# Seven block products for two output classes of an MLP's second product, with their differences on GpSimd

## The chip, the core and the metric

The kernel runs on one core of a Trainium2 chip. The core has a matrix engine (TensorE, PE in the profile; its weight loads are PEld), a vector engine (VectorE, DVE), an activation engine (ScalarE, ACT), GpSimd (POOL) and a queue engine for transfers (SyncE, SP). They run side by side; each takes its own instructions strictly in the order in which they are written, and an instruction that needs another engine's result waits on a semaphore. TensorE reads SBUF and accumulates in PSUM, which has eight banks of 512 float32 columns; VectorE and ScalarE read PSUM, GpSimd does not.

The metric is the device time of one execution in microseconds. All data are float32.

## The reference

The input is 16 images of 192 channels and 64 x 64 pixels. Cut to what matters here:

```python
h  = ln2d(x)                                   # over channels
projected, gate = split(conv1x1(h, in_proj))   # 192 -> 2 x 192
projected = dwconv3(projected)
mixed = (scan_4_directions(projected) + dwconv3(projected)) * sigmoid(gate)
x = x + conv1x1(gelu(batchnorm(mixed)), out_proj)
h2 = ln2d(x)
m = conv1x1(gelu(conv1x1(h2, fc1) + b1), fc2) + b2    # 192 -> 768 -> 192
x = x + m                                      # "the image"
# second layer: per-image 3x3 taps of which 4 are unmasked
pooled = mean(x, axis=(2, 3))
taps = relu(norm(pooled @ w1.T)) @ w2.T + b2
out = depthwise_conv3x3(x, taps per image and channel, masked) + bias
```

The change concerns `conv1x1(gelu(...), fc2)`, the second MLP product, and the buffers that hold the image between it and the last convolution.

## The kernel before

The kernel has three stages. The first normalizes and projects the input, the second runs the depthwise convolutions and scans channel by channel, the third does everything from the batch norm on. The order of all instructions on all engines is the order in which the program writes them; no scheduler moves anything.

**Layout of the third stage.** Two images are worked on at once, one on partitions 0 to 63 and one on 64 to 127 (`HALF`). The 192 channels are three classes of 64 (`t` = 0, 1, 2). A step `n` handles one chunk of 512 pixels (8 rows) of a pair of images; a pair has 8 steps, there are 8 pairs, 64 steps in all. In a step, the loop at L1141 writes work of four different chunks: the MLP of chunk `n`, the normalization of `n + 1`, the out-projection of `n + 2`, and the unmixing (transposes) and Gelu of the mixed data of `n + 3`.

**The MLP.** `first` (L965) makes one of six blocks of 128 hidden channels: twelve matmuls of 64 x 64 weights and 512 columns into a tile of two PSUM banks (tag `f1`, two such tiles), then ScalarE's Gelu into an SBUF tile `gl` of 128 x 2 x 512 (six of them). `second` (L978) multiplies the six blocks with the three classes of `wf2`, 128 x 64 weights and 512 columns per image, through `both` (L840): 36 matmuls in a step. Each float32 matmul has two records in the profile, so 72. They accumulate in three PSUM banks (tag `f2`). `final` (L991), at the start of the next step, adds each class with its bias to the image on VectorE (L997) and lets the same instruction sum the pixels for the pooling.

**The normalization.** `residual` (L900) adds out-projection, bias and input into the image and collects channel sums (L910, L921). `mean`, `center`, `squares` and `normalize` produce `h`, the MLP's input: two matmuls against a constant matrix, a subtraction (L941), ScalarE's squares (L949) and their sums on VectorE (L950, L921), a square root on ScalarE (L959), a reciprocal (L962) and a scaling (L963) on VectorE.

**The last convolution.** When a pair has ended, its taps are computed (`pooled`, `squeeze`, `excite`) and its twelve pieces (four bands of 16 rows x three classes) are put on a list. `piece()` (L1075) takes one: ScalarE does the first tap (L1034), VectorE three more (L65), and GpSimd's queue stores the result (L1038). It is called twice a step, so the pieces of one pair fill the first six steps of the next.

**Buffers.** The images are held in two tiles `ximg` of 3 x 65 x 66 values a partition, one per pair in turn; row 0 and the side columns are zeros (`border`, L817). The second tile first serves as room for mixed data (`spare`, `ys`).

The order within a step of before: `final(n-1)`, `first` 0 and 1, `mean` and `center`, `first` 2, `squares`, `first` 3 and 4, `unmix`, `load_mixed`, a piece, `first` 5, the out-projection's matmuls (L890, L897) mixed with the second `mean`, `residual` of class 1, `normalize`, `residual` of 0 and 2, Gelu of the mixed data, `second`, with the second piece inside it. `second`'s order of matmuls is written at L985 to L989:

```python
order = [(m, t) for m in gl for t in range(3)]
for m, t in order:
    both(s["po"][t], lambda i: wf2[:, m, 64 * t:64 * t + 64], lambda i: gl[m][:, i], m == 0, m == NFC - 1)
```

Of the kernel before, what the change touches and what calls it, by code (L numbers as in the profile page):

```python
# [27 lines left out]
C = 192  # L28
# [27 lines left out]
def conv_block_kernel(ctx: ExitStack, tc: tile.TileContext, x, prm, w_in, w_out, w_fc1, b_fc1, w_fc2, w1, bn1, w2, out):  # L56
# [756 lines left out]
    n_img = 2  # L813

    ximg = [k3.tile([128, 3, HW + 1, RW], F32, tag=f"ximg{i}", name=f"ximg{i}") for i in (1, 0)][::-1]

    def border(xi):  # L817
        nc.gpsimd.memset(xi[:, :, 0:1], 0.0)
        nc.gpsimd.memset(xi[:, :, :, 0:1], 0.0)
        nc.gpsimd.memset(xi[:, :, :, RW - 1:RW], 0.0)  # L820


    spare = ximg[1].rearrange("p t h w -> p (t h w)")
    ys = {n // 2: spare[:, (n - 2) * 3 * CH:n * 3 * CH].rearrange("p (t w e) -> p t w e", t=3, w=2) for n in range(2, NCH, 2)}
    ys[0] = y_low
# [5 lines left out]
    wp = ctx.enter_context(tc.tile_pool(name="w2", bufs=1))  # L831
# [4 lines left out]
    NPS = NFC // 2  # L836
# [3 lines left out]
    def both(ps, w, rhs, start, stop):  # L840

        for i, q in enumerate(HALF):
            nc.tensor.matmul(ps[q], w(i), rhs(i), start=start, stop=stop)  # L843

    def img_of(n):
        r = 1 + (n % NCH) * CR
        return ximg[(n // NCH) % n_img][:, :, r:r + CR, 1:1 + HW]
# [52 lines left out]
    def residual(n, t, ps):  # L900
# [4 lines left out]
        if n == 0:  # L905
            return
        s["added"] = s.get("added", ()) + (t,)
        if t < 2 and len(s["added"]) == 2:
            s["sum"] = hp2.tile([128, 3, HCH], F32, tag="sm", name="sm", bufs=1)
            nc.vector.tensor_add(rows(s["sum"][:, 0:2].rearrange("p k n -> p (k n)")), img[:, 0], img[:, 1])  # L910
        if t == 2:
            sm = s["sum"]
            s["sm"] = [sm[:, j] for j in range(3)]
            sums(*(rows(sm[:, j]) for j in (0, 1, 2, 0, 1)), img[:, 2, 0:CR // 2], img[:, 2, CR // 2:CR])
# [30 lines left out]
    def squares(n):  # L945
# [3 lines left out]
        nc.scalar.activation(sq, s["h"], AF.Square)  # L949
        nc.vector.tensor_add(sq[:, 0], sq[:, 0], sq[:, 1])  # L950
# [4 lines left out]
    def normalize(n):  # L955
        s = st[n]
# [6 lines left out]
        nc.vector.tensor_mul(s["h"], s["h"], rs.unsqueeze(1).broadcast_to([128, 3, CH]))  # L963
# [14 lines left out]
    def second(n, k):  # L978
        s = st[n]
        gl = {m: s.pop(("gl", m)) for m in (2 * k, 2 * k + 1)}  # L980
        if k == 0:
            po = [ps2.tile([128, CH], F32, tag="f2", name="ps_f2", bufs=3) for _ in range(3)]

            s["po"] = po[1:] + po[:1]
            order = [(m, t) for t in range(3) for m in gl]  # L985
        else:
            order = [(m, t) for m in gl for t in range(3)]
        for m, t in order:
            both(s["po"][t], lambda i: wf2[:, m, 64 * t:64 * t + 64], lambda i: gl[m][:, i], m == 0, m == NFC - 1)  # L989

    def final(n):  # L991
        p, c = divmod(n, NCH)
        if c == 0:
            pst[p]["sums"] = hp2.tile([128, 3, NCH], F32, tag="sums", name="sums")
        img = img_of(n)
        for t in range(3):
            nc.vector.scalar_tensor_tensor(img[:, t], rows(st[n]["po"][t]), pt3[:, t, FC2B:FC2B + 1], img[:, t],  # L997
                                           ALU.add, ALU.add, accum_out=pst[p]["sums"][:, t, c:c + 1])
        st[n].clear()
# [27 lines left out]
    def dynamic(p, g, t):  # L1027
        xi, taps, r = ximg[p % n_img], pst[p]["taps"], g * GR
        o = op.tile([128, GR, HW], F32, tag="o", name="o")
        for k in range(NTAP):  # L1030
            src = xi[:, t, r + k // 3:r + k // 3 + GR, k % 3:k % 3 + HW]
            w = taps[:, t, k:k + 1]
            if k == 0:
                nc.scalar.activation(o, src, AF.Identity, bias=pt3[:, t, BIAS:BIAS + 1], scale=w)  # L1034
            else:
                stt(o, src, w, o)
        for i, q in enumerate(HALF):
            nc.gpsimd.dma_start(ov[2 * p + i, 64 * t:64 * t + 64, r * HW:(r + GR) * HW], o[q].rearrange("p h w -> p (h w)"))  # L1038

    def dynamic_last(p, r, nr, t, dg, o=None, queues=(nc.gpsimd, nc.sync)):  # L1040

        xi, taps, hr = ximg[p % n_img], pst[p]["taps"], nr // 2
        src = lambda k, r0, n: xi[:, t, r0 + k // 3:r0 + k // 3 + n, k % 3:k % 3 + HW]
# [29 lines left out]
    pieces = []  # L1073

    def piece():  # L1075
        if pieces:
            dynamic(*pieces.pop(0))
# [29 lines left out]
    border(ximg[0])  # L1107
# [29 lines left out]
    out_alone(1, 2)  # L1137
    idle(1)


    for n in range(n_ch + 1):  # L1141
        ended = (n - 1) // NCH if n >= NCH and (n - 1) % NCH == NCH - 1 else None
# [7 lines left out]
        if n == 1:  # L1150
            load_y(6, ys[3], (nc.gpsimd,))
        if n == NCH - 3:
            border(ximg[1])
        at(first, n, 0)
        at(first, n, 1)
# [4 lines left out]
        if n == 0:  # L1160
            unmix(2)
        at(first, n, 2)
        at(squares, n + 1)
        for m in range(3, NFC - 1):
            at(first, n, m)
            if n == 0 and m == 3:
                bn_gelu(2)
        at(unmix, n + 3)
        at(load_mixed, n + 4)
        piece()  # L1170
        at(first, n, NFC - 1)
# [21 lines left out]
        at(normalize, n + 1)  # L1193
        if po:
            for t in (0, 2):
                residual(n + 2, t, po[t])
        at(bn_gelu, n + 3)
        at(second, n, 0)
# [4 lines left out]
        at(second, n, 1)  # L1203
        piece()
# [77 lines left out]
```

## Time and profile before

| | |
|---|---|
| median of three runs | 3676.18 us (3673.29 to 3678.82) |
| profiled execution | span 3672.7 us from first to last instruction; its own time outside the span is not shown apart |
| third stage | from about 1328 us to the end, 64 steps |
| one step | 35.96 us |
| one step, busy | TensorE 35.96, VectorE 26.75, ScalarE 15.77, GpSimd 2.13 us |
| mean granted TensorE clock | 0.998 of full speed |

How the rows are read. A row of the groups has line, engine and operation, output <- inputs with shapes, the count, then busy microseconds and mean nanoseconds of one, then the engine's idle time before it and what ended it. A row of the timeline has start and length in microseconds, then the same. Matmul rows overlap each other (several run at once in different parts of the array), so the time of a run of matmuls is read from its start to the start of the row after it. The view of stages has for each window its length, and each engine's busy time with the number of instructions.

### The profile page before, as it was taken

The numbers are of one execution on the slowest core, as the hardware profiler recorded it, in microseconds if no ns is written. First come the engines' busy times: TensorE is split into PE (matmuls) and PEld (weight loads), VectorE is DVE, ScalarE is ACT, GpSimd is POOL, SyncE is SP. The second block draws the span as 40 slices with busy tenths as digits, with TensorE's granted clock in tenths as the row PEclk, the third lists the DMA queues.
The fourth block names the chain that finished last, engine by engine and source line by source line (L and its number), as shares of the span: only waits on it lengthen the run. The fifth ranks groups of instructions, "written<-read, shape, count | busy, mean of one in ns | idle before, by whom it ended". The sixth has DMA issues, their size and how long they took to land.

```text
span 3672.7 us, 71322 instructions
## 1 busy us (share of the span) xinstructions
PE 3649.8 (99%) x30354; PEld 1724.1 (47%) x30354; DVE 2713.3 (74%) x4138; ACT 1792.0 (49%) x2004; POOL 419.3 (11%) x685
## 2 busy tenths in 40 slices
PE   9999999999999999999999999999999999999998
PEld 6666666555566643343343334333334334333334
DVE  7878776999999965557757767776766775775764
ACT  3343434988888843334443534343444434343533
POOL 3434332111111120000000000000000000000000
PEclk9999999999999999999999999999999999999999
DMA  7898998999999951022212212222222231222212
GB/s 172 243 251 247 264 278 245 300 297 290 280 279 288 250 104 37 25 60 66 78 47 81 75 47 67 81 61 53 77 71 55 65 85 47 75 69 61 73 38 75
DMA packets 290334, 491.81 MB, mean 134 GB/s; under 512 B 26584, under 2 KB 184784, under 8 KB 290016
## 3 DMA queue, kind: packets, MB, share of 16 engines
q1 hardware_dynamic: 232540, 296.22, 30.2%
q0 software_dynamic: 56544, 189.99, 18.7%
q8 instruction: 239, 3.92, 0.5%
q10 hardware_dynamic: 932, 1.03, 0.1%
q14 instruction: 79, 0.65, 0.1%
HBM read 284.95 MB, written 197.92 MB: 131 GB/s over the span
## 4 chain that ended last, share of the span: by engine, by line
PE 90%; DVE 1%; DMA 0%; issue 0%; ACT 0%; ACTq 0%; SPq 0%; POOL 0%; DVEq 0%
PE ps_f L973 27%; PE ps_f L843 27%; PE ps_l L673 11%; PE ps_pj L514 7%; PE ps_d L629 7%; PE ps_o L897 5%; PE ps_o L890 2%; PE ps_xt L485 1%; PE ps_m L929 1%; PE ps_v L929 1%; PE ps_k L843 0%; DMA xa<-in_x_dram 0%; DVE o L65 0%; PE pb_h L141 0%; DVE ol L65 0%
## 5 line engine op out<-in xcount | busy, mean ns | idle before, releaser
L975 ACT ACTIVATE gl<-ps_f,bf 128x1024 f32<-128x1024 f32 x384 | 428.0, 1115 | 1298.5 <-PE ps_f L973 1292.8
L973 PE MATMUL ps_f<-h,wf 64*64 64x512 f32 x9216 | 1014.9, 590 | 2.0 <-DVE h L963 2.0
L843 PE MATMUL ps_f<-gl,place 128*64 128x512 f32 x4608 | 1001.9, 592 | 0.8 <-ACT rs L959 0.8
L973 PEld LDWEIGHTS ps_f<-h,wf 64*64 64x64 f32 x9216 | 346.3, 133 | 627.9 <-issue 566.0
L843 PEld LDWEIGHTS ps_f<-gl,place 128*64 128x64 f32 x4608 | 334.9, 137 | 623.8 <-issue 613.9
L514 PE MATMUL ps_pj<-wi,xa 64*128 64x384 f32 x3072 | 514.7, 487 | 1.7 <-DVE stg L519 1.2
L514 PEld LDWEIGHTS ps_pj<-wi,xa 64*128 64x128 f32 x3072 | 292.0, 187 | 196.0 <-issue 10.6
L65 DVE SCALAR_TENSOR_TENSOR o<-ximg,taps,o 128x1024 f32<-128x1024 f32 (+1 forms) x267 | 336.5, 1261 | 22.5 <-ACT o L1034 14.1
L941 DVE TENSOR_TENSOR h<-ximg,ps_m 128x768 f32<-128x768 f32 x128 | 116.4, 951 | 308.2 <-PE ps_m L929 307.0
L1038 POOL DMA_DIRECT2D out_dram<-o x168 | 89.8, 539 | 2012.5 <-DVE o L65 2009.7
L997 DVE SCALAR_TENSOR_TENSOR ximg<-ps_f,pt,ximg 128x512 f32<-128x512 f32 x192 | 144.4, 752 | 173.1 <-PE ps_f L843 160.4
L664 DVE TENSOR_TENSOR_SCAN v<-tab,q 128x1024 f32<-128x1024 f32 x96 | 218.3, 2274 | 7.8 <-ACT tab L652 7.8
L962 DVE RECIPROCAL rs<-rs 128x512 f32<-128x512 f32 x64 | 214.1, 3346 | 5.3 <-ACT rs L959 5.2
L666 DVE TENSOR_TENSOR_SCAN v<-tab,q 128x1024 f32<-128x1024 f32 x96 | 217.6, 2266 | 0.0
L520 ACT ACTIVATE mid<-ps_pj,rsa 128x384 f32<-128x384 f32 x128 | 120.2, 940 | 184.2 <-PE ps_pj L514 178.8
L652 ACT ACTIVATE tab<-mask,dec_b 128x1024 f32<-128x1024 f32 x192 | 209.8, 1146 | 0.0
L520 ACT ACTIVATE stg<-ps_pj,rsa 128x384 f32<-128x384 f32 x128 | 120.0, 941 | 180.4 <-PE ps_pj L514 172.9
L950 DVE TENSOR_TENSOR low<-low 128x512 f32<-128x512 f32 x63 | 43.6, 693 | 209.2 <-ACT low L949 209.2
L903 DVE SCALAR_TENSOR_TENSOR ximg<-ps_o,pt,low 128x256 f32<-128x256 f32 x384 | 168.1, 478 | 30.5 <-PE ps_o L897 28.0
L492 DVE BATCH_NORM_STATS2 st<-ps_xt 128x6 f32<-128x192 f32 x512 | 173.9, 340 | 13.8 <-PE ps_xt L485 13.0
L897 PE MATMUL ps_o<-low,wo 128*64 128x256 f32 x1536 | 182.0, 385 | 0.2 <-ACT low L870 0.2
L243 DVE STREAM_TRANSPOSE low<-low 128x512 f32<-128x512 f32 x174 | 170.0, 1029 | 2.0 <-issue 0.3
(213 smaller groups left out, 4186.1 us busy)
## 6 DMA issues: line engine op xcount, KB each, us to landing
low<-in_x_dram SPq DMA_DIRECT2D x128, 384.0 KB
out_dram<-o POOLq DMA_DIRECT2D x168, 256.0 KB, 4.6
mid<-pg_d SPq DMA_DIRECT2D x8, 4096.0 KB
low<-mixed_d SPq DMA_DIRECT2D x116, 256.0 KB
low<-pg_d SPq DMA_DIRECT2D x7, 4096.0 KB
pg_o<-pg_d SPq DMA_DIRECT2D x7, 4096.0 KB
xa<-in_x_dram POOLq DMA_DIRECT2D x192, 128.0 KB, 5.6
xa<-in_x_dram SPq DMA_DIRECT2D x192, 128.0 KB
```

Of the source, the lines that this page charges most:

```text
L65: nc.vector.scalar_tensor_tensor(o, in0, scalar, in1, ALU.mult, ALU.add, **kw)
L514: nc.tensor.matmul(ps[i], pixels(n, t, g)[q], wi[q, t].rearrange("p g k c -> p (g k c)"), start=(t == 0), stop=(t == 2))
L520: nc.scalar.activation(stag[blk][1][:, :, j], ps[1], AF.Copy, scale=rs[:, g, 1:2])
L629: nc.tensor.matmul(dst(ps[o, ih]), mats[g % 2]["dm"][q, di + 1, :, ch], src(s["pg"][q, :, 0, ch]), start=(di == 0), stop=stop)
L664: nc.vector.tensor_tensor_scan(vf, tab, q, 0.0, ALU.mult, ALU.add)
L666: nc.vector.tensor_tensor_scan(vf[:, ::-1], tab[:, ::-1], q[:, ::-1], 0.0, ALU.mult, ALU.add)
L673: nc.tensor.matmul(dst(bst[k]["ps"][o, i]), lm_of(g)[q, m, :, c], src(q, ih), start=start, stop=stop)
L843: nc.tensor.matmul(ps[q], w(i), rhs(i), start=start, stop=stop)
L897: nc.tensor.matmul(ps[wh][q].rearrange("p (r w) -> p r w", w=32), wo[:, 64 * t:64 * t + 64], cols(rows(s["mx"][:, i]))[:, :, wh], start=fi ...
L962: nc.vector.reciprocal(rs, rs)
L973: nc.tensor.matmul(pf[o, i], wf1[q, t, m0:m0 + 64], s["h"][q, t], start=(t == 0), stop=(t == 2))
L975: nc.scalar.activation(gl, pf, AF.Gelu, bias=bf1[:, m:m + 1])
```

## The change

The two output classes 0 and 1, with the hidden blocks 0 to 2 and 3 to 5 and the two halves of the 512 pixels, are written as a product of 2 x 2 block matrices, weights [[a11, a12], [a21, a22]] by hidden values [[b11, b12], [b21, b22]], in seven block products instead of eight (Winograd's form of Strassen's method). Class 2 stays as it was (`last_tile`).

- **Weights.** `sums_of_weights` makes four sums of weight blocks once, on GpSimd, before the first step.
- **Differences.** `differences` makes four differences of hidden blocks a step, each in three instructions of 128 x 512 on GpSimd: t1 = b12 - b11 and t2 = b22 - t1 while `first` makes the blocks; b12 = b22 - b12, in place, once the first half of class 2 has read it; b21 = b21 - t2, in place, once products 2 and the second half of class 2 have read it.
- **Products.** `seven` runs one block product: three blocks x two images, 256 columns. Products 1, 6, 7 and 4 accumulate in one bank (`chain`), which VectorE reads between them: 1 into class 0 left, 1+6 into class 0 right, 1+6+7 into class 1 right, 1+6+7+4 into class 1 left. Products 5, 2 and 3 use the two halves of a tile of the tag `f1`.
- **Additions.** `onto` adds a product to the image on VectorE: seven of 256 columns and one of 512 in place of three of 512.
- **Order.** `first` makes blocks 0, 3, 1, 4, 2, 5. `unmix` and `load_mixed` move to the start of the step, `residual` loses its channel sums to `add_up`, which comes after class 2's second half; `squares` and `normalize` are cut in two (`add_squares`; `spread_root` and `scale`). A piece's first tap on ScalarE comes at the end of the step before (`begin`), two or one in turn; its other taps come after blocks 0 and 4. The stores go to SP's queue.
- **Buffers.** Instead of two whole images, six slots of 17 rows (one row above and a band of 16) are used in turn; after each band GpSimd copies its last row to the top of the next slot, and `top` clears the first.

The order of `second` and the differences, cut from the diff (`n` is the step; the rest of the moves is told above):

```diff
+    def differences(n, m, kind):
+        b11, b12, b21, b22 = (quarter(n, k, x) for k, x in ((0, 0), (0, 1), (1, 0), (1, 1)))
+        if kind == 1:
+            sub(t1[:, m], b12(m), b11(m))
+        elif kind == 2:
+            sub(t2[:, m], b22(m), t1[:, m])
+        elif kind == 3:
+            sub(b12(m), b22(m), b12(m))
+        else:
+            sub(b21(m), b21(m), t2[:, m])
+
+    def seven(n, j, ps, start=False):
+        src = {1: quarter(n, 0, 0), 2: quarter(n, 1, 0), 3: quarter(n, 1, 1), 4: quarter(n, 1, 0),
+               5: lambda m: t1[:, m], 6: lambda m: t2[:, m], 7: quarter(n, 0, 1)}[j]
+        for m in range(NPS):
+            both(ps, lambda i: wsum[j][:, m], lambda i: src(m)[:, i], start and m == 0, m == NPS - 1, skip_group_check=True)
+
+    def onto(n, t, x, ps, bias=False, last=False):
...
+        if bias:
+            nc.vector.scalar_tensor_tensor(img, rows(ps), pt3[:, t, FC2B:FC2B + 1], img, ALU.add, ALU.add, **acc)
+        elif last:
+            nc.vector.scalar_tensor_tensor(img, rows(ps), 1.0, img, ALU.mult, ALU.add, **acc)
...
+    def second(n):
...
+        chain, whole = [ps2.tile([128, CH], F32, tag="f2", name="ps_f2", bufs=3) for _ in range(2)]
+        two = ps2.tile([128, 2, CH], F32, tag="f1", name="ps_s", bufs=2)
+        chain, left, right = chain[:, 0:HCH], two[:, 0, 0:HCH], two[:, 1, 0:HCH]
+        seven(n, 1, chain, True)
+        onto(n, 0, 0, chain, bias=True)
+        yield
+        last_tile(n, whole, 0)
+        for m in range(NPS):
+            differences(n, m, 3)
+        yield
+        seven(n, 5, right, True)
+        onto(n, 1, 1, right, bias=True)
+        seven(n, 6, chain)
+        onto(n, 0, 1, chain, bias=True)
+        seven(n, 2, left, True)
+        onto(n, 0, 0, left, last=True)
+        last_tile(n, whole, 1)
+        for m in range(NPS):
+            differences(n, m, 4)
+        if n + 2 < n_ch:
+            add_up(n + 2)
+        yield
+        onto(n, 2, None, whole, bias=True, last=True)
+        seven(n, 7, chain)
+        onto(n, 1, 1, chain, last=True)
+        seven(n, 3, right)
+        onto(n, 0, 1, right, last=True)
+        seven(n, 4, chain)
+        yield
...
     for n in range(n_ch + 1):
         at(final, n - 1)
...
+        at(unmix, n + 3 if n else None)
+        at(load_mixed, n + 4)
         at(first, n, 0)
+        at(differences, n, 0, 1)
+        piece()
+        at(first, n, NPS)
+        at(differences, n, 0, 2)
             mean(n + 1, pm, "sm")
             center(n + 1, pm)
+        at(first, n, 1)
+        at(squares, n + 1)
+        at(differences, n, 1, 1)
+        at(first, n, NPS + 1)
+        at(differences, n, 1, 2)
+        at(add_squares, n + 1)
+        piece()
         at(first, n, 2)
+        at(differences, n, 2, 1)
+        at(first, n, NPS + 2)
+        at(differences, n, 2, 2)
...
+        at(spread_root, n + 1)
+        steps = second(n) if n < n_ch else iter(())
+        next(steps, None)
+        at(scale, n + 1)
         if po:
             for t in (0, 2):
                 residual(n + 2, t, po[t])
+        next(steps, None)
         at(bn_gelu, n + 3)
...
+        next(steps, None)
+        begin(2 if c % 2 == 0 or n == n_ch - 3 else 1)
+        next(steps, None)
```

In the changed kernel `first`'s matmuls are L992, its Gelu L994, `both` is L851 (so the seven products and class 2), `onto` L1045 (with bias) and L1047, `differences` L1018, L1020, L1022 and L1024, `residual` L912, the reciprocal L977, the scaling L982.

## The prediction, made before the changed kernel was run

> **What bounds the kernel now.** I read the busy times first, then the chain of work that ended last, then TensorE's rows in order of time for one step of the third stage (a step is one group of 512 pixels of two images), and last that step's VectorE and GpSimd rows.
>
> ```profile
> PE 3649.8 (99%) x30354; PEld 1724.1 (47%) x30354; DVE 2713.3 (74%) x4138; ACT 1792.0 (49%) x2004; POOL 419.3 (11%) x685
> PE 90%; DVE 1%; DMA 0%; issue 0%; ACT 0%; ACTq 0%; SPq 0%; POOL 0%; DVEq 0%
> ```
>
> TensorE is the bound from end to end, so only a change in its own work or a new wait of TensorE moves the time. The stage runs from 1328 to 3673 us as 64 steps. One step by engine (length, then PE, PEld, DVE, ACT, POOL, granted clock, DMA share, GB/s), and TensorE's rows around it:
>
> ```profile
> 2036.00:2071.96 35.96, 35.96 (x283) 13.75 (x281) 26.75 (x36) 15.77 (x17) 2.13 (x4) 1.00 0.20 50
> ```
> ```profile
> 2033.36 2.81 PE L897 MATMUL ps_o<-low,wo 128*64 128x256 f32 x24
> 2036.00 15.62 PE L843 MATMUL ps_f<-gl,place 128*64 128x512 f32 x72
> 2051.55 5.38 PE L973 MATMUL ps_f<-h,wf 64*64 64x512 f32 x48
> 2056.75 0.61 PE L929 MATMUL ps_m<-sm,mean 64*64 64x256 f32 x8
> ```
>
> The reader is to see that each row begins where the one before it hands over: a step is 35.96 us of TensorE without a gap. The second product (L843) takes 2051.55 - 2036.00 = 15.55 us for 72 records of 512 columns, 0.216 each; 24 records of 256 columns with the same weight shape (L897) take 2036.00 - 2033.36 = 2.64, 0.110 each. VectorE is busy 26.75 of 35.96 us, GpSimd only issues DMAs. The VectorE rows just after L897, and its dearest rows with two SBUF inputs:
>
> ```profile
> 2071.77 0.87 DVE L903 SCALAR_TENSOR_TENSOR ximg<-ps_o,pt,low 128x256 f32<-128x256 f32 x2
> 2072.56 3.34 DVE L962 RECIPROCAL rs<-rs 128x512 f32<-128x512 f32 x1
> 2075.94 1.76 DVE L963 TENSOR_TENSOR h<-h,rs 128x1536 f32<-128x1536 f32 x1
> 2077.61 0.87 DVE L903 SCALAR_TENSOR_TENSOR ximg<-ps_o,pt,low 128x256 f32<-128x256 f32 x2
> ```
> ```profile
> L65 DVE SCALAR_TENSOR_TENSOR o<-ximg,taps,o 128x1024 f32<-128x1024 f32 x13 | 16.6, 1280 | 0.4
> L921 DVE TENSOR_TENSOR low<-low 64x256 f32<-64x256 f32 x8 | 3.4, 420 | 0.3
> L910 DVE TENSOR_TENSOR sm<-ximg 128x512 f32<-128x512 f32 x2 | 1.4, 694 | 0.1
> ```
>
> Today nothing waits for this order: the second product that follows needs only the hidden blocks.
>
> **The change, part by part.** Times below count from the first matmul of a step.
>
> (a) TensorE's work. Out go 48 of the 72 records of classes 0 and 1 (24 x 2, at 0.216: 10.37 us). In come seven products of 3 blocks x 2 halves x 2 records = 84 records of 256 columns, at L897's 0.110: 9.24. Class 2 keeps 24 x 0.216 = 5.18. Saved: 1.13 us a step, 72 us in all; a step is 34.83 us of TensorE.
>
> (b) A new wait inside the seven. Out-projection columns end at 20.4. Then product 1 (1.32) to 21.7, half of class 2 (2.59) to 24.3, product 5 to 25.6, product 6 to 26.95, product 2. Product 2 writes the tile that product 5 used, so it waits until VectorE has added product 5 to the image. VectorE's queue before that: the second square root ends 19.5 into the step (before: 2071.05 - 2051.55); reciprocal 19.8 to 23.15; adding product 1 0.42 (the two L903 rows of the same size take 2072.56 - 2071.77 = 0.79 start to start); scaling h 1.70; four residuals 1.70; adding product 5 0.42: 27.4, and 0.1 to hand over. TensorE waits 27.5 - 26.95 = 0.55. There is no slack here: whatever delays this queue delays TensorE one for one. Without anything further the gain is 1.13 - 0.55 = 0.58 a step, 37 us in 64.
>
> (c) VectorE's total. Three additions of L997 (752 + 84 ns, 2.5 us) become seven of 256 columns (about 0.48) and one of 512, five with the 84 ns read of the accumulator: 4.5 us. With a step's two image pieces that is 26.75 + 2.0 = 28.8; pieces come two and one in turn, so the mean is 27. It fits in 35 if nothing stretches it.
>
> (d) GpSimd's twelve differences a step, 128 x 512 with two SBUF inputs. No row of before shows one. The nearest:
>
> ```profile
> masks.py:199 POOL TENSOR_SCALAR_AFFINE_SELECT ident<-ident 128x128 f32<-128x128 f32 x1 | 0.3, 287 | 0.1
> masks.py:197 POOL MEMSET ident<- 128x128 f32 x1 | 0.2, 205 | 0.3 <-POOLq L1272 0.3
> L391 POOL MEMSET wf<- 24x1024 f32 x8 | 7.6, 947 | 0.3
> ```
>
> The memsets rise (947 - 205)/896 = 0.83 ns an element, so 0.52 us for 512 written elements is the low end; four times the select, which reads and writes, is 1.15, and I take that, since a difference reads twice. Twelve are 13.8 us of a 35 us step. Alone they are hidden: t1 and t2 finish by 18.8 and products 5 and 6 begin at 24.3; the last three start when class 2's second half has read their block, about 30.1, end at 33.5, and product 4 needs the last at 34.9. This cover lasts up to 1.6 us a difference.
>
> (e) GpSimd beside VectorE. In a step VectorE's instructions with two SBUF inputs are the taps (1.28 each, six or three), scaling (1.76), the sums of squares and of h's input (2.4 each): 14.2 us with two pieces, 10.3 with one. No row of before shows one of them beside a GpSimd instruction that reads SBUF. The bounds are nothing, and strict turns, where each of the two waits for the other's end. (A gain from meeting is excluded: neither does less.) The rows lean to nothing: the 24x1024 memset beside VectorE's PSUM reads keeps 944 to 952 ns, and VectorE's taps keep 1229 to 1286 beside ScalarE and TensorE; but neither is a pair of this kind. I take strict turns, because the result hangs on so little: 0.58 us in (b)'s queue ends the gain, that is half of one difference, and the three differences on classes 0 and 1's first block start at 23.0, just ahead of scaling in that queue.
>
> The Trainium skill speaks against the change here. Its page "SBUF — State Buffer", section "SBUF: two separate sides", says that VectorE and GpSimd share one pair of ports, locked for a whole instruction, and names VectorE instructions with two SBUF inputs against GpSimd ones that read SBUF. No row here shows it; by the rule the sum is the strict turns below, by the rows' lean it is 37 us less than before.
>
> Strict turns, the rows laid end to end at 1.15 a difference. A step with two pieces: two differences come between the three taps of the first piece (+2.3), so centring ends at 11.8 instead of 9.6; ScalarE's squares are queued behind it, ahead of the fourth block's Gelu, which now ends at 14.5 instead of 12.3, and TensorE's sixth block waits 1.25 for its PSUM. Two more come between the taps of the second piece (+2.3): the reciprocal starts at 22.95 instead of 19.8, scaling loses 0.9, and product 2 waits 3.4. The sums of h's input lose 1.15, so product 4 waits 0.9 for the chain's bank. Together 5.55 of waits on 34.83: 40.4, 4.45 above 35.96. With one piece the middle wait is 1.1: 38.1, +2.1; at the pairs' first and last steps +1.3 and +1.1; the first eight steps have no pieces, +0.9. So 28 x 4.45 + 14 x 2.1 + 7 x 1.3 + 7 x 1.1 + 8 x 0.9 = 178, less about 4 at the end, where steps thin out: 174.
>
> (f) Edits at nothing. The output stores go from GpSimd's queue to SP's, two per piece: 84 of 0.54 us issue there, 45 us of a queue that nothing computes on; behind them on SP stand the loads of x2 and mixed, needed a step later; those waited for VectorE up to 32 us already. If they came late, the transposes at the start of the step would. Weight sums (four on GpSimd, under 0.5 each) lie beside the out-projections before step 0. Row copies and borders: one each second step, under 0.55. Ring slots instead of two images: addresses only.
>
> **Sum.** The profiled execution spans 3672.7; the three timed runs have 3673.29, 3676.18 and 3678.82, so the span lies 3.5 below the median. 3672.7 + 174 + 3.5 = 3850.
>
> **Rivals.**
> Faster: differences and VectorE run beside each other, (d) hidden, (b) alone counts: 3676 - 37 = 3639. It speaks for it that no row shows a stretch; against, that 0.58 us of delay decides it. Chance 0.33.
> Nearly free: short differences in turns. At 0.52 us the same laying gives +3.5, so 3680; the point where it turns slower. Chance 0.05 within 0.2%.
> GpSimd is the bound: without turns, above 1.6 us a difference product 4 waits; at 1.8, 36.1 a step, 3684; at 2.0, 3723. The rows above say 1.15 at most. Chance 0.04.
> GpSimd first at every meeting: taps wait each time, VectorE loses 9.8 us a step, 42.8: 4100. Chance 0.06.
> The products do not get cheaper: 256 columns at 0.1235 a record would eat (a); then (b) leaves 3676 + 35 = 3711. L897's 0.110 speaks against. Chance 0.02.
> The forecast, turns at some price between 3690 and 3960: 0.50.
>
> **How the numbers follow.** A difference of 0.2% (7 us) is about what a measurement of this kernel can tell from no change. Slower 0.50 + 0.06 + 0.04 + 0.02 = 0.62, same 0.05, faster 0.33. The likeliest case alone spans 3720 (0.65 us a difference) to 3960 (1.4 us). Both signs hold much, so the range reaches from the free case, 3630, to 3960; it leaves out the GpSimd-first case and the forecast's tails.
>
> **What would show it.** L851's 256-column records at 0.110 and a TensorE total some 70 us lower show (a). Waits of L851 for L1045 of about 35 us in all show (b) alone; 120 or more, together with taps far above 1286 ns or gaps before them that end with GpSimd's, show (e). GpSimd's rows give (d). Wrong would be: taps and scaling unchanged beside differences, or differences that VectorE never meets.

## The result and the profile after

The changed kernel takes 3882.0 us (median of four runs, 3874.5 to 3887.4) against 3676.5 us before on the same chip: 1.056 times as long, with a 95% interval from 1.054 to 1.057. That is 206 us more, 32 us above the forecast of 3850. One execution further below, the profiled one of the early differences alone, ran at a granted clock of 0.594 from end to end and took 7766.6 us; it stands in no comparison, and none of its rows is used.

The busy times of the changed kernel's page and, below them, the shares of the chain that ended last:

```profile
PE 3667.8 (94%) x32658; PEld 1884.0 (48%) x32658; DVE 3229.1 (83%) x4594; ACT 1793.5 (46%) x2004; POOL 1430.9 (37%) x1319
PE 51%; DVE 34%; issue 4%; ACT 2%; DMA 0%; POOL 0%; SPq 0%; DVEq 0%; ACTq 0%
```

Before, TensorE was 99% busy and 90% of the chain. Now a third of the chain is VectorE's, whose busy time rose by 3229.1 - 2713.3 = 516 us (78 of them come with the rest of the change: the kernel without differences, below, has 2791.3). GpSimd, which does the new work, has none of the chain: its time is paid on another engine.

A step with two image pieces, one with one piece, and one of the first eight, which have none (stretch; its length, then PE, PEld, DVE, ACT, POOL, granted clock, DMA share, GB/s):

```profile
2390.60:2431.05 40.45, 37.31 (x319) 16.69 (x317) 35.55 (x42) 14.64 (x15) 16.58 (x13) 0.96 0.19 47
2431.05:2469.45 38.40, 35.82 (x318) 16.43 (x316) 31.77 (x39) 15.88 (x16) 17.36 (x12) 1.00 0.26 76
1400.00:1437.74 37.74, 35.17 (x320) 16.30 (x318) 24.97 (x37) 13.51 (x14) 17.50 (x13) 1.00 0.09 22
```

All three were 35.96 us before. The first is among the shortest of its kind: the 26 steps with two pieces in which TensorE waits 3.1 us before product 2 take 40.5 to 42.2 us, 41.0 on the mean. The waits of TensorE between 1600 and 3800 us (engine, line and tile that waited; whom for; total us, times, longest):

```profile
PE ps_s L851 <- DVE ximg L1045: 62.0, 31, 3.2
PE ps_f L851 <- DVE ximg L1047: 44.4, 24, 1.9
PE ps_s L851 <- DVE spare L1045: 36.4, 17, 3.2
PE ps_f L851 <- DVE spare L1047: 27.8, 15, 1.9
```

The first and third rows are product 2, which waits for the addition of product 5; the others are product 4, which waits for the addition of product 7. VectorE's and GpSimd's groups show what made those additions late (the first number after the bar is busy us, then mean ns of one):

```profile
L65 DVE SCALAR_TENSOR_TENSOR o<-ximg,taps,o 128x1024 f32<-128x1024 f32 x180 | 315.7, 1755 | 5.0
L927 DVE TENSOR_TENSOR low<-low 64x256 f32<-64x256 f32 x252 | 216.6, 860 | 8.0
L927 DVE TENSOR_TENSOR sm<-sm,ximg 64x256 f32<-64x256 f32 x172 | 183.7, 1068 | 3.3
L982 DVE TENSOR_TENSOR h<-h,rs 128x1536 f32<-128x1536 f32 x64 | 174.1, 2721 | 0.0
L1022 POOL TENSOR_TENSOR gl<-gl 128x512 f32<-128x512 f32 x192 | 294.1, 1560 | 266.0 <-PE ps_f L851 266.0
```

Taps went from 1280 to 1755 ns, the additions of 64x256 from 420 to 860 and 1068, the scaling of h from about 1.76 us to 2.72. Nothing about these instructions changed; all have two inputs in SBUF. VectorE's instructions with a PSUM input kept their times, and so did the reciprocal, which has one input in SBUF (3344 ns). A difference on GpSimd takes about 1.27 us when nothing hinders it (1260 ns at its shortest), with means up to 1560. Two meetings, the scaling of each of two consecutive steps and then GpSimd's three differences beside it:

```profile
2416.65 2.78 DVE L982 TENSOR_TENSOR h<-h,rs 128x1536 f32<-128x1536 f32 x1
2454.57 2.85 DVE L982 TENSOR_TENSOR h<-h,rs 128x1536 f32<-128x1536 f32 x1
```
```profile
2414.07 3.74 POOL L1022 TENSOR_TENSOR gl<-gl 128x512 f32<-128x512 f32 x3 [4.09 <-PE ps_f L851]
2454.54 5.25 POOL L1022 TENSOR_TENSOR gl<-gl 128x512 f32<-128x512 f32 x3 [4.57 <-PE ps_f L851]
```

In the first meeting the scaling starts 1.16 us before the differences end (at 2417.81). It takes 1.03 us longer than its 1.75, while the differences keep their time, 3.74 us for three. So the one that comes later waits, and the earlier one is not slowed: the two do not share a rate. In the second, GpSimd's first difference starts 0.03 us before the scaling. The scaling takes 1.1 us longer, nearly one difference, and the three differences take 5.25 us instead of 3.74, the missing 1.5 being most of a scaling. Each waited for the other once. The wait lies inside the row: it is counted as busy time, not as idle time, and only the length of the row gives it away.

### The profile page after: what moved, and what is told of

Its sections match the earlier page's. It is cut to its first block, busy times and chain, and to the rows that moved or that the text cites. A ratio compares the mean times of both kernels' runs of the same rounds, so it can differ in the third digit from the quotient of the medians.

```text
span 3885.4 us, 77607 instructions
## 1 busy us (share of the span) xinstructions
PE 3667.8 (94%) x32658; PEld 1884.0 (48%) x32658; DVE 3229.1 (83%) x4594; ACT 1793.5 (46%) x2004; POOL 1430.9 (37%) x1319
## 3 DMA queue, kind: packets, MB, share of 16 engines
q10 hardware_dynamic: 932, 1.03, 0.1%
## 4 chain that ended last, share of the span: by engine, by line
PE 51%; DVE 34%; issue 4%; ACT 2%; DMA 0%; POOL 0%; SPq 0%; DVEq 0%; ACTq 0%
PE ps_f L992 13%; PE ps_l L673 11%; DVE o L65 7%; PE ps_pj L514 7%; PE ps_d L629 7%; PE ps_f L851 6%; DVE sm L927 5%; DVE rs L977 5%; PE ps_s L851 4%; DVE h L982 3%; DVE low L927 2%; DVE ximg L912 2%; DVE low L243 2%; DVE ximg L1045 1%; DVE h L947 1%
## 5 line engine op out<-in xcount | busy, mean ns | idle before, releaser
L994 ACT ACTIVATE gl<-ps_f,bf 128x1024 f32<-128x1024 f32 x384 | 426.6, 1112 | 1359.8 <-PE ps_f L992 1336.0
L992 PE MATMUL ps_f<-h,wf 64*64 64x512 f32 x9216 | 1023.4, 592 | 3.9 <-DVE h L982 2.0
L992 PEld LDWEIGHTS ps_f<-h,wf 64*64 64x64 f32 x9216 | 342.2, 133 | 615.6 <-issue 563.9
L851 PE MATMUL ps_f<-gl,place 128*64 128x256 f32 (+1 forms) x3072 | 551.4, 501 | 87.2 <-DVE ximg L1047 57.5
L1018 POOL TENSOR_TENSOR t<-gl 128x512 f32<-128x512 f32 x192 | 271.0, 1412 | 527.3 <-ACT gl L994 525.4
L851 PEld LDWEIGHTS ps_f<-gl,place 128*64 128x64 f32 x3072 | 235.1, 141 | 331.9 <-issue 272.9
L1022 POOL TENSOR_TENSOR gl<-gl 128x512 f32<-128x512 f32 x192 | 294.1, 1560 | 266.0 <-PE ps_f L851 266.0
L1020 POOL TENSOR_TENSOR t<-gl,t 128x512 f32<-128x512 f32 x192 | 268.0, 1396 | 294.2 <-ACT gl L994 294.2
L1024 POOL TENSOR_TENSOR gl<-gl,t 128x512 f32<-128x512 f32 x192 | 262.7, 1395 | 280.4 <-PE ps_f L851 280.1
L65 DVE SCALAR_TENSOR_TENSOR o<-ximg,taps,o 128x1024 f32<-128x1024 f32 x180 | 315.7, 1755 | 5.0
L473 POOL DMA_DIRECT2D xa<-in_x_dram x192 | 120.5, 636 | 362.5 <-PE ps_pj L514 325.4
L927 DVE TENSOR_TENSOR low<-low 64x256 f32<-64x256 f32 x252 | 216.6, 860 | 8.0
L977 DVE RECIPROCAL rs<-rs 128x512 f32<-128x512 f32 x64 | 214.0, 3344 | 5.5 <-ACT rs L974 5.5
L851 PE MATMUL ps_s<-gl,place 128*64 128x256 f32 x768 | 113.6, 438 | 104.1 <-DVE ximg L1045 67.7
L927 DVE TENSOR_TENSOR sm<-sm,ximg 64x256 f32<-64x256 f32 x172 | 183.7, 1068 | 3.3
```

The costliest lines, as they stand in the source:

```text
L65: nc.vector.scalar_tensor_tensor(o, in0, scalar, in1, ALU.mult, ALU.add, **kw)
L927: nc.vector.tensor_add(o, a, b)
L977: nc.vector.reciprocal(rs, rs)
L992: nc.tensor.matmul(pf[o, i], wf1[q, t, m0:m0 + 64], s["h"][q, t], start=(t == 0), stop=(t == 2))
L994: nc.scalar.activation(gl, pf, AF.Gelu, bias=bf1[:, m:m + 1])
L1018: sub(t1[:, m], b12(m), b11(m))
```

## The experiments

Theory: VectorE's instructions with two SBUF inputs and GpSimd's differences take strict turns; VectorE's queue gets longer, and TensorE waits for it at products 2 and 4. Rivals: the new order of `second` itself waits (product 2 behind VectorE's longer queue, 256-column products); any GpSimd work costs; the differences are simply too slow.

### Without the differences

```diff
     def differences(n, m, kind):
+        return
```

> The changed kernel with the twelve differences a step left out (both difference buffers are zeroed once and the products read them as they are, so the second product of the two classes is not the reference's); all else stays. Theory of turns (VectorE's instructions with two SBUF inputs and GpSimd's differences wait for one another): nothing is left to meet, so the whole loss and the whole of what the change should have brought come back, 3640 us (3620 to 3665), the scaling back at 1.76 us from a median of 2.78, a two-piece step at 35.5 us from 40.45. Rival, the new order itself (product 2 behind VectorE's longer queue, 256-column products, clock): 3850 to 3880, the waits for ps_s and ps_f as they are, 3.1 and 0.7 to 1.9 us a step.

Measured: 3600.7 us (3599.8 to 3604.2), 0.980 of before (0.978 to 0.981). Two consecutive steps, one without and one with two full sets of taps:

```profile
2376.15:2410.93 34.78, 34.78 (x319) 16.24 (x317) 24.18 (x39) 15.88 (x16) 0.26 (x1) 1.00 0.29 84
2410.93:2445.71 34.78, 34.78 (x318) 16.24 (x317) 28.04 (x42) 14.64 (x15) 0.00 (x0) 1.00 0.22 55
```
```profile
L65 DVE SCALAR_TENSOR_TENSOR o<-ximg,taps,o 128x1024 f32<-128x1024 f32 x180 | 229.7, 1277 | 4.9
L984 DVE TENSOR_TENSOR h<-h,rs 128x1536 f32<-128x1536 f32 x64 | 111.9, 1749 | 0.0
```

TensorE fills the step again, and taps and scaling have their old times. The differences cost 3882 - 3601 = 281 us, and the rest of the change brings 75. The rival of the order falls. The expectation's 3640 was 39 too high: product 2 does not wait here at all. VectorE ends the addition of product 5 at 2402.97, 26.82 us into the step, and product 6 ends at 26.9.

### GpSimd writes as long, but reads nothing

```diff
-    sub = nc.gpsimd.tensor_sub
+    def sub(o, a, b):
+        for w_ in (HCH, HCH, HCH // 2):
+            nc.gpsimd.memset(o[:, :, 0:w_], 0.0)
```

> Each difference replaced by three memsets of the same output (512, 512 and 256 elements; by the 0.95 us of a memset of 24x1024 about 1.2 us together), so GpSimd writes as long, in the same places, behind the same waits, but reads nothing; the products are not the reference's. Theory of turns as the prediction put it (GpSimd's instruction reads SBUF): 3640 us (3620 to 3670), the scaling at 1.76 us. Rival 1, any GpSimd instruction on SBUF takes a turn: 3860 to 3890, the scaling still at 2.5 or more. Rival 2, waits of TensorE and ScalarE for GpSimd's late results rather than VectorE's stretching: at least half of the loss stays, 3760 or more, with the scaling at 1.76.

Measured: 3604.4 us (3601.6 to 3607.5). GpSimd's and VectorE's groups:

```profile
L1014 POOL MEMSET gl<- 128x512 f32 x768 | 403.6, 526 | 1107.6 <-PE ps_f L851 1068.1 <-ACT low L880 17.3
L1014 POOL MEMSET gl<- 128x256 f32 x384 | 120.0, 313 | 22.1
L982 DVE TENSOR_TENSOR h<-h,rs 128x1536 f32<-128x1536 f32 x64 | 111.9, 1748 | 0.0
```

Two memsets of 526 ns and one of 313 are 1.37 us in place of each difference, more than its 1.27, in the same places and behind the same waits, and they cost 3.7 us in all. So neither GpSimd's time nor waits for its results matter, and its writes meet nobody. What is left is what the difference does and the memset does not: it reads SBUF (and computes; no run separates the two). The Trainium skill's page "SBUF — State Buffer", section "SBUF: two separate sides", says that it is the reading: a VectorE instruction with two SBUF inputs is held only against a GpSimd instruction that reads SBUF. These two runs agree, with 281 us against 4.

### Differences of half the width

```diff
-    sub = nc.gpsimd.tensor_sub
+    def sub(o, a, b):
+        nc.gpsimd.tensor_sub(*(v[:, :, 0:HCH // 2] for v in (o, a, b)))
```

> Differences over half of their columns (256 elements, about 0.65 us by half of 1.27; the other half of the products' operands is not the reference's). Theory of turns, with VectorE's slack of some 3 to 5 us a step taking the first part: 3700 us (3670 to 3745), less than half of the way from 3640 to 3882. If the cost goes by GpSimd's time in proportion: 3760. If each meeting costs a fixed turn whatever the length: 3850 or more.

Measured: 3651.2 us (3647.0 to 3653.2), 50.6 above the kernel without differences. A difference of 256 elements takes 721 ns at its shortest: half the elements, 57% of the time, 18% of the cost. The scaling's mean is 2047 ns, the taps' 1400. The cost is far from proportional: VectorE is busy 148 us longer than without differences (2939.4 against 2791.3), but the time grows by only 51, and steps with and without taps are all 35.6 us. The stretching of the taps disappears in VectorE's slack. Even the low end of what was expected was 19 too high, because the expectation started from 3640 instead of 3601.

### The scaling with one input in PSUM

```diff
-        nc.vector.reciprocal(rs, rs)
-        s["rs"] = rs
+        inv = ps2.tile([128, CH], F32, tag="a", name="ps_r")
+        nc.vector.reciprocal(inv, rs)
+        s["rs"] = inv
```

> Nothing of the computation changes: the reciprocal is written into PSUM and the scaling reads it there, so that the scaling has one input in SBUF. Theory of turns: the scaling goes from a median of 2.78 us to 1.76 (1.7 to 1.9) though the differences beside it stay, the wait for ps_s in product 2 falls by about 1 us a step where the scaling ended it, total 3855 us (3835 to 3870). Rival, any VectorE instruction that reads SBUF takes turns, or the stretch is contention by bandwidth: scaling stays at 2.5 us or more, total 3875 to 3890.

Measured: 3851.6 us (3848.1 to 3858.0), 30.5 less than the changed kernel. VectorE's scaling and taps:

```profile
L983 DVE TENSOR_TENSOR h<-h,ps_r 128x1536 f32<-128x1536 f32 x64 | 111.5, 1742 | 0.0
L65 DVE SCALAR_TENSOR_TENSOR o<-ximg,taps,o 128x1024 f32<-128x1024 f32 x180 | 315.9, 1756 | 4.9
```

The same scaling beside the same differences has its 1742 ns back, while the taps stay stretched. This shows the other half of the rule: it is the second SBUF input, not reading SBUF as such, that makes VectorE take turns. (Shared bandwidth would ease too when one input leaves SBUF; what speaks against that is the first of the two meetings above, in which the differences are not slowed.) Both sides of the theory now have a run of their own.

### Only the early, only the late differences

```diff
     def differences(n, m, kind):
+        if kind not in (1, 2):       # the second run: (3, 4)
+            return
```

> Of the twelve differences a step only the six that run beside the first products are kept (t1 and t2); the two kinds that overwrite gl beside the second products are left out, so products 4 and 7 read what the reference's would not. Theory of turns: the scaling and the sixth block's sums no longer meet anything late in the step: the scaling at 1.76 us, the taps and the squares' sums (low) as stretched as in the changed kernel (1.75 and 0.86 us); 3735 us (3690 to 3775), that is about half of the 281 us between 3601 and 3882. Rival, only the late meetings cost (the wait for ps_s in product 2 is the one that the waits show): 3605 to 3640.

> Only the six differences beside the second products are kept (kinds 3 and 4, from t2 zeroed once); t1 and t2 are not computed. Theory of turns: taps and squares' sums back to 1.28 and 0.42 us, the scaling at 2.5 us or more; no difference left between one- and two-piece steps; 3720 us (3680 to 3765). Rival, only the late meetings cost: 3840 to 3880, nearly the whole loss.

Measured: the early ones alone 3717.9 to 3722.4 us in three executions; the late ones alone 3784.6 us (3782.7 to 3787.6). Against 3601 the early six cost 118 us and the late six 184, each alone; together they cost 281, a little less than the sum. The rival by which only the late ones count falls; the expected even split does too. In the run of the late ones the steps with and without taps are all 37.8 us, which is the 37.74 of the changed kernel's steps without pieces. So the late meetings cost each of the 64 steps 3 us, and the early ones cost only where taps run. VectorE's scaling and the sums of h's input in that run, which carry it:

```profile
L984 DVE TENSOR_TENSOR h<-h,rs 128x1536 f32<-128x1536 f32 x64 | 169.1, 2642 | 0.0
L929 DVE TENSOR_TENSOR sm<-sm,ximg 64x256 f32<-64x256 f32 x172 | 195.1, 1134 | 3.3
```

### t1 and t2 on VectorE

```diff
+        sub = (nc.vector if kind in (1, 2) else nc.gpsimd).tensor_sub
```

> The computation is the reference's: the changed kernel with the six differences t1 and t2 on VectorE instead of GpSimd. VectorE gains 6 times about 0.69 us (its 128x512 addition in SBUF), 4.1 us a step. Theory of turns: six of twelve meetings go, the late ones, worth 184 us alone, stay; VectorE's 4.1 us lie in its queue ahead of the scaling: 3855 us (3830 to 3880), little below the 3882 of the changed kernel. If VectorE has room for them: 3785 to 3800, the time of the kernel that leaves t1 and t2 out. If VectorE becomes the bound: 3890 or more.

Measured: 3882.5 us (3879.9 to 3889.4), the time of the changed kernel and 27 above the expectation. The taps have their 1283 ns back, but VectorE does six more instructions a step:

```profile
L1017 DVE TENSOR_TENSOR t<-gl 128x512 f32<-128x512 f32 x192 | 132.3, 689 | 53.3 <-ACT gl L994 51.4
L1019 DVE TENSOR_TENSOR t<-gl,t 128x512 f32<-128x512 f32 x192 | 133.4, 695 | 164.3 <-ACT gl L994 160.7
```

Those are 4.15 us a step ahead of the reciprocal; a step with two pieces is 40.2 to 42.3 us, mostly 40.6, and one with one piece 38.2. Handing the work to the engine that is late is no better than letting it be stretched.

### Another order: first product 2 ahead of the reads

`second`'s matmuls and additions (scaling and residuals stay where they were, between product 1's addition and class 2's first half):

```diff
         seven(n, 5, right, True)
+        seven(n, 2, left, True)
         onto(n, 1, 1, right, bias=True)
+        onto(n, 0, 0, left, last=True)
         seven(n, 6, chain)
         onto(n, 0, 1, chain, bias=True)
-        seven(n, 2, left, True)
-        onto(n, 0, 0, left, last=True)
```

> Nothing of the computation changes; product 2 is issued straight behind product 5, ahead of VectorE's addition of product 5, so TensorE no longer waits for that addition before product 2 and its next wait for VectorE is one product later. Where turns lengthen VectorE and the loss comes through that wait: the wait for ps_s in product 2 (3.1 us a step) goes, part of it returns at the products behind; 3810 us (3780 to 3845). Rival, VectorE itself is the bound of the step (its own queue, not the place of the wait): 3865 to 3890. Rival, the wait is the whole loss in the late half: 3740 to 3780.

Measured: 3798.8 us (3797.2 to 3799.7), 83 less than the changed kernel. The waits of TensorE between 1600 and 3700 us:

```profile
PE ps_f L851 <- DVE ximg L1047: 77.2, 35, 2.6
PE ps_f L851 <- DVE spare L1047: 44.2, 20, 2.5
```

The 98 us of waits at product 2 are gone; those at product 4 grew from 72 to 121, now 55 of them. A wait was removed and part of it came back one product later, in front of the addition that stands behind the stretched sums (`sm`). This left the question whether an order exists that hides the rest.

### One block of three, in that order

The outer two of the three pairs of blocks are summed by plain products into the accumulators that exist; only the middle pair needs differences.

```diff
+    MS, REST = (1,), (0, 2)
     def seven(n, j, ps, start=False):
-        for m in range(NPS):
+        for m in MS:
+    def plain(n, j, x, ps):
+        for m in REST:
+            for k in range(2):
+                both(ps, lambda i: wsum[j][k][:, m], lambda i: quarter(n, k, x)(m)[:, i], ...)
         seven(n, 5, right, True)
+        plain(n, "10", 1, right)
```

(The same after products 2, 3 and 4; for product 3 with differences of the weights, since its accumulator already holds the other class.)

> The computation is the reference's. The order of the run before, and seven products only for the middle one of the three pairs of blocks (four differences a step instead of twelve, 24 more records of 256 columns saved only where they were: TensorE saves a third of 1.17 us, 0.39 a step or 25 us); the other two pairs are summed by plain products into the same accumulators, two of them with differences of the weights. Theory of turns with slack (half the time of differences cost 50 us, the whole 281): four differences in places where VectorE has room cost 5 us or less, 3655 us (3640 to 3670), faster than both. Rival, cost in proportion to GpSimd's time (94 us for a third): 3735 to 3755.

Measured: 3695.1 us (3693.1 to 3696.7), 1.0048 of before (1.0035 to 1.006): a miss of 40. Steps are 36.22 us with taps and without (a pair's first step, which computes the taps, is 38.12; it was 37.87 before). TensorE's and VectorE's rows at its end:

```profile
2380.43 2.33 PE L851 MATMUL ps_s<-gl,ws 128*64 128x256 f32 x20
2383.17 2.38 PE L851 MATMUL ps_f<-gl,place 128*64 128x256 f32 x20 [0.41 <-DVE ximg L1058]
```
```profile
2379.07 2.82 DVE L927 TENSOR_TENSOR sm<-sm,ximg 64x256 f32<-64x256 f32 x4
2381.92 0.75 DVE L1056 SCALAR_TENSOR_TENSOR ximg<-ps_f,pt,ximg 128x512 f32<-128x512 f32 x1
2382.60 0.42 DVE L1058 SCALAR_TENSOR_TENSOR ximg<-ps_f,ximg 128x256 f32<-128x256 f32 x1
```

TensorE waits at one place, product 4, for the addition of product 7 at 2382.60; that stands behind class 2's addition and the sums of the next image's h, which took 2.82 us instead of 1.72 beside one difference. The wait is 0.58 us with the hand-over, and without it a step would be 35.64. That is also the least that one block can reach: it needs 92 records of 256 columns, 8 more than the kernel without differences, so 0.86 us on top of 34.78.

### The order mended: scaling and sums moved behind

```diff
         onto(n, 0, 0, chain, bias=True)
-        between[0]()                 # scaling
         between[1]()                 # residuals of classes 0 and 2
+        between[0]()
 ...
-        if n + 2 < n_ch:
-            add_up(n + 2)            # the sums of h's input
         yield
         onto(n, 2, None, whole, bias=True, last=True)
         seven(n, 7, chain)
         onto(n, 1, 1, chain, last=True)
+        if n + 2 < n_ch:
+            add_up(n + 2)
```

> The computation is the reference's, with all twelve differences. Beside product 2 ahead of the reads, the scaling stands behind the two residuals, and the sums of the images (sm) stand behind the addition of product 7, where TensorE no longer waits for what is queued behind them. Theory of turns: VectorE stays as stretched (scaling and taps at 2.5 and 1.7 us), but what is stretched lies ahead of fewer waits of TensorE; steps without taps reach 34.8 us, those with taps 36.5 to 37: 3690 us (3665 to 3725), 110 less than the order with product 2 moved alone. Rival, VectorE and GpSimd together are the bound of a step and no order helps: 3780 to 3810.

Measured: 3673.7 us (3668.7 to 3676.1), 0.9988 of before (0.9979 to 0.9998), with all twelve differences; 208 us less than the changed kernel, by order alone. The rival that the two engines are the bound whatever the order falls. A step with two pieces and one without; then VectorE's sums of h's input:

```profile
2373.12:2409.41 36.29, 35.49 (x319) 16.47 (x317) 32.68 (x43) 14.53 (x15) 16.80 (x12) 1.00 0.21 52
1400.00:1434.72 34.72, 34.72 (x318) 16.33 (x316) 22.18 (x37) 13.50 (x14) 17.16 (x13) 1.00 0.11 25
```
```profile
L927 DVE TENSOR_TENSOR sm<-sm,ximg 64x256 f32<-64x256 f32 x172 | 72.4, 421 | 3.3
```

Without taps the whole gain is there. The sums of 64x256 now come when GpSimd has finished, and are not stretched, and the scaling takes 2138 ns on the mean instead of 2721. VectorE is busy 3051.6 us instead of 3229.1, and 165 of these 178 us are the sums. So the expectation had the time right, but only part of the reason: it left VectorE as stretched as before, while the new order also took meetings away. What is left, 1.57 us in the steps with taps, lies in the first half, where t1 and t2 meet the taps. The sums now stand ahead of the taps, which begin 4.2 us into the step instead of 3.3 as in the changed kernel, and the squares and Gelus behind them come 0.9 us later too. TensorE waits there for ScalarE's Gelu, which frees the PSUM tile of the next block:

```profile
PE ps_f L992 <- ACT gl L994: 36.7, 46, 0.8
```

That is 0.8 us in 46 steps, 1.9 us in all in the changed kernel; it is the only wait of TensorE that returns from step to step. Most of the rest (0.53) stands at the second `mean`, whose row takes 0.93 us instead of 0.61, as in the changed kernel.

### Two blocks of three in the mended order

`MS, REST = (1, 2), (0,)` in the mended order.

> The computation is the reference's. The order of the run before, and seven products for the second and third of the three pairs of blocks (eight differences a step), the first pair summed by plain products. TensorE saves two thirds of 1.17 us a step, 50 us in all. Theory of turns with slack: without the first pair's differences, which fall on the taps, nothing stretched reaches a wait of TensorE: 3635 us (3615 to 3665), faster than before. Rival, the cost goes by the time of the differences (two thirds of what twelve cost in this order): within 15 us of the run before this one, and above 3670.

Measured: 3626.8 us (3625.7 to 3627.9), 0.9864 of before (0.985 to 0.9879), 50 us faster than the kernel before and 255 faster than the changed one. Two consecutive steps, the second with two pieces, and the taps:

```profile
2388.92:2424.08 35.16, 35.16 (x322) 16.62 (x321) 26.40 (x40) 15.88 (x16) 10.86 (x10) 1.00 0.29 83
2424.08:2459.24 35.16, 35.16 (x323) 16.62 (x321) 30.63 (x43) 14.64 (x15) 11.57 (x8) 1.00 0.21 54
```
```profile
L65 DVE SCALAR_TENSOR_TENSOR o<-ximg,taps,o 128x1024 f32<-128x1024 f32 x180 | 265.5, 1476 | 4.9
```

TensorE has no gap in either step. The taps are still stretched by 0.2 us each on the mean, and it costs nothing: steps without taps are 35.16 us too. No run leaves out another pair of blocks, so how much of this is the place of the first pair's differences, and how much that there are fewer, is not shown apart. Leaving out the first pair's differences costs 0.43 us of TensorE in each step (four records more) and frees the 1.57 of a step with taps.

## Why the prediction was right, and where it was not

**(a) TensorE's work: right.** The 256-column records take 0.108 us against 0.110 predicted, and a step without waits is 34.78 us against 34.83.

**(b) The new wait at product 2: wrong by its whole size.** Predicted 0.55 us a step, measured none in the kernel without differences. Each small term was rounded up: the reciprocal starts 19.5 us into the step instead of 19.8, the addition of product 1 takes 0.30 from start to start instead of 0.42, the four residuals 1.57 instead of 1.70. The addition of product 5 so ends at 26.82 instead of 27.4, just ahead of product 6's end, and the whole wait is gone. The place was right, and that it has no slack; but the free case was 3601 and not 3639, below the low end of the range. What the change could bring was therefore twice what the prediction thought at stake.

**(c) VectorE's total: right within 3%.** Without meetings it is busy 28.04 us in a step with two pieces against 28.8.

**(d) The difference: 10% short.** 1.27 us against 1.15: four times the select's 287 ns came near, but it was no upper bound, as the rival on GpSimd took it ("1.15 at most"). From 256 to 512 elements the shortest grows by 539 ns, 2.1 ns an element. That it is hidden by itself is shown by the run with memsets.

**(e) Strict turns: right**, and taken against the lean of the rows; the runs without differences, with memsets and with the PSUM input show it. A step with two pieces was forecast at 40.4. The one shown takes 40.45, but by other parts, so this agreement is luck; the 26 take 41.0 on the mean. Against the kernel without differences, the middle of the step shown loses 0.66 us instead of 1.25, and most of that (0.54) is not at the sixth block but at the second `mean`, which waits for the stretched sums of squares. Product 2 starts 3.31 later through its own wait, forecast 3.4; but 0.55 of the 3.4 was (b)'s wait, which is not there without differences, so the turns alone cost 3.31 against 2.85. Product 4 does not wait in this step. In its place class 2's second half and product 2 run 1.7 us longer at a lower clock, which was not foreseen. A step with one piece was forecast at 38.1 and takes 38.40: 0.67 in the middle, 0.86 at product 2 and 2.05 at product 4. The first eight were forecast at 36.9 and take 37.74: 0.86 and 2.05. The term that was most short is product 4's 0.9. In the steps where it waits, the four sums of h's input meet three differences and take about 4.65 us instead of 1.72, not one difference and 1.15 more, and product 4 starts 2.05 late. From the first step's start to the 64th's, the mean step is 39.46 us against 36.13 before. That is 210 of the 213 us by which the two profiled executions differ; the medians differ by 206, 32 more than the 174 summed. The sign named for (e) did not come as named: the waits of L851 for L1045 are 104 us in all, not 120 or more, and another 85 us are waits for L1047 at product 4. The sign for (a), a TensorE total some 70 us lower, shows only in the kernel without differences (3574.5 us, 75 less); in the changed kernel it is 3667.8, 18 more than before.

**(f) Edits at nothing: right.** The kernel without differences keeps the ring, the stores on SP's queue, the weight sums and the row copies, and no gap of TensorE is left in its steps. Two of its numbers were off, with nothing hanging on them: the page of before shows 168 stores on GpSimd's queue and 89.8 us, not 84 and 45, and a sum of weights takes 0.6 us, not under 0.5.

**Rivals.** The free case's mechanism falls with the stretched rows. The case of short differences had its turning point wrong for the same reason as (b): at 721 ns the kernel is 25 us faster than before, where the prediction had 3720 for 0.65 us. GpSimd as the bound falls with the memsets, which take longer than the differences and cost 3.7 us; GpSimd first at every meeting falls with the second of the two meetings shown, where a difference waits for the scaling; products that do not get cheaper fall with the 0.108. That the time came within 32 us is in part luck, because the errors had opposite signs: no wait for (b), more at product 4.

## What to carry to other kernels

Before work goes to an idle GpSimd, list VectorE's instructions with two SBUF inputs that run at the same time, add one GpSimd instruction to each, and look which wait of the bounding engine stands behind them. Order decides as much as amount: the same twelve differences cost 281 us or 73 over the kernel without them, depending on how many meet a VectorE instruction and whether the stretched ones stand ahead of an addition that TensorE needs; at half their width, in the first order, they cost 51. And where a stretch is hidden up to a point, a part of the change can be worth more than the whole: two of three blocks were 47 us faster than three in the same order.

## What the runs showed that was not expected

Turns are counted as busy time. VectorE's share rose from 74% to 83% and no idle time before the scaling tells of it; a reader who looks at idle time alone sees an engine that got busier.

TensorE's granted clock can fall after a wait. After the wait of 3.13 us before product 2, the stretches of product 2 and of class 2's second half read (clock in the third number from the end):

```profile
2421.44:2422.91 1.47, 1.47 (x12) 0.93 (x14) 0.34 (x1) 0.00 (x0) 0.00 (x0) 0.91 0.00 0
2422.91:2427.06 4.15, 4.15 (x14) 1.26 (x12) 3.81 (x7) 0.00 (x0) 1.89 (x2) 0.62 0.02 6
2460.79:2463.40 2.61, 2.61 (x16) 0.89 (x14) 2.36 (x4) 0.87 (x1) 1.49 (x2) 1.00 0.03 9
```

The third row is the work of the second after a wait of 0.69 us. Of the 26 such waits of 3.1 us in the changed kernel, 21 were followed by longer rows and five were not; after waits of 1.9 us no work took more than 0.05 us longer. It costs little here: in the five cases at full clock the step took 40.9 us, since product 4 then waited 1.9 us for VectorE instead, and in the 21 others 41.0 on the mean. What decides whether the clock falls after such a wait stays open.
